# Graph network with mixtures of experts: the begins of four stages rearranged

## The chip, the cores and the metric

The kernel runs on one core of a Trainium2 chip. A core has five engines that run side by side, each taking its own instructions in order: TensorE (PE) multiplies matrices and transposes tiles, VectorE (DVE) and ScalarE (ACT) work element by element, GpSimd (POOL) issues the indirect DMAs (gathers) here, and SyncE (SP) issues most of the other DMAs; ACT and POOL have DMA queues too. PE writes to PSUM; DVE and ACT bring results from there to SBUF. The metric is the device time of one execution in microseconds (us), lower is better.

## What is computed

The input is x, 3125 nodes by 256 channels, with 50,000 edges (source, destination, one of eight types, a weight). Eight blocks follow each other, each with a residual connection and a layer norm ahead of it:

```python
x = x + L0_gnn(norm(x))      # attention over edges
x = x + L0_ffn(norm(x))      # slices and attention over them
x = x + L1_gnn(norm(x))      # four graph convolutions, 256-128-64-128-256
x = x + L1_ffn(norm(x))      # two of 16 experts per node, then a norm
x = x + L2_gnn(norm(x))      # two blocks norm-convolution-relu, then x @ Wp.T + bp
x = x + L2_ffn(norm(x))      # a shared MLP and two of 4 experts
x = x + L3_gnn(norm(x))      # relational convolution, eight edge types
x = x + L3_ffn(norm(x))      # one of 8 experts, with a capacity
```

The four convolutions of L1 gnn each form `segment_sum(h[src] * dinv[src] * dinv[dst], dst) + b`. L1 ffn, where the change has its largest part:

```python
gate_logits = x @ gate_w + gate_b
topk_vals, topk_idx = jax.lax.top_k(gate_logits, K)          # K = 2
topk_w = jax.nn.softmax(topk_vals, axis=-1)
h = jax.nn.relu(jnp.einsum('bsh,ehf->bsef', x, w1) + b1)     # 16 experts, 256 -> 512
expert_out = jnp.einsum('bsef,efh->bseh', h, w2) + b2        # 512 -> 256
sel = jnp.take_along_axis(expert_out, topk_idx[:, :, :, None], axis=2)
y = x + jnp.sum(topk_w[..., None] * sel, axis=2)
return (y - mu) / jnp.sqrt(var + EPS) * gamma + beta
```

L3 gnn forms `h_all = einsum('ni,roi->rno', node, weight)` and sums `h_all[type, src]` by destination.

## The kernel before

Nodes lie in 25 tiles (NT) of 128 (P); x stays in SBUF as 128x25x256 floats, D = 256 channels, KC = 2 chunks of 128. Many loops run over groups of five tiles (SG). A framework's scheduler sets the order of instructions on each engine and the waits between engines; the program text does not fix it, but work that depends on nothing late can be drawn forward. Stages follow each other in time: L0 up to about 400 us, the building of an edge-count table (cells) up to 720, L1 gnn 724 to 1114, L1 ffn 1114 to 1502, L2 gnn 1504 to 2250, L2 ffn to 2420, L3 gnn to 3057, L3 ffn to the end. Pools of SBUF tiles are opened and closed by stage, and a new pool's tile can only be written once its addresses' old users are done. `evict` (L103 to L105) copies PSUM to SBUF and takes ACT and DVE in turn, call by call.

L1 gnn (`l1_gnn`, L1066 to L1131). The biases b1 to b4 are loaded through SP's queue, and right after them five DVE additions add b4 to all of x (L1074). Then four calls of `aggregate` follow. In each, a tile takes 25 PE matmuls with the edge counts (L1081, PSUM tile `agg`), a DVE reduction over the three bf16 parts (L1084, `s`), and then the stage's `finish`: after1 scales and adds b1, transposes (L1090, `tr`), applies relu on ACT (L1092), multiplies by w2 and splits into three bf16 parts; after4 scales (L1123), transposes, multiplies by w4 (L1125) and adds the product to x (L1126). While a tile's finish runs, PE goes on with the next tile's matmuls.

L1 ffn (`l1_ffn`, L1154 to L1317). The expert weights w1 and w2 (16.8 MB) are loaded through SP (L1179, L1182). Then the front, by groups of five tiles (from L1186): layer norm, a store of the normed rows to the DRAM table `tab_x1` through POOL's queue (L1190), transposes (L1195), `by_node` matmuls with the gate's weights (L563), and an addition of the gate's bias into `lg` (L1199). Then routing on DVE: `top_two` (L591 to L615), counting, and the owners of the slots. Between, beta is added to x (L1247). Then the work on experts: a gather of 128 rows per slot from `tab_x1` (L681, `xg`), transposes (L1262), two layers of matmuls (L1268, L1281) and a store to `yb`.

L2 gnn (`l2_gnn`, L1325 to L1424). The weights W6, W7 and Wp are loaded into two buffers `w_o`, transposed (L1335) and copied by `evict`. Then, for each group of five tiles, `input_group` (the function `combined` of L1 ffn) loads y from `tab_x1` through SP (L1295), gathers two expert rows per tile from `yb` through POOL (`yg`, three buffers each), folds them into y (L1303), norms, and adds to x (L1311, L1313); after it `first_input` norms, transposes and multiplies by W6. The adjacency tables `adj` (1.6 MB each, L517) are loaded through SP.

L3 gnn (`l3_gnn`, L1645 to L1719). For each block of 128 edges: a gather of source rows (L681, `g`), a DVE comparison that makes a 0/1 matrix (`hot`, L1703), and PE matmuls that sum the rows by destination and type (L1708, `sum`). DVE adds each sum into a ring of destinations in SBUF (`acc`, 128x8576 floats, L1714). When a tile of destinations is complete, ACT copies it out and clears its place by a copy from `zero` (L1664, L1665), and PE multiplies it by the weights (L1685); then the front of L3 ffn follows for that tile (`l3_ffn_front`: layer norm, `f_tr`, `f_xT`, `f_mm`). At the stage's begin DVE clears `zero` (L1654) and the whole ring (L1657).

## Time and profile before

| what | us |
|---|---|
| runs before, median of 3 (lowest, highest) | 3270.08 (3268.21, 3270.93) |
| the profiled execution | 3264.51 |
| its span on the core | 3262.6 |

| engine | busy us | share of the span |
|---|---|---|
| PE (matmul) | 2693.3 | 83% |
| DVE | 1408.6 | 43% |
| ACT | 871.3 | 27% |
| POOL | 632.8 | 19% |

The busy shares are averages over stages with different limits, so the stage's own rows decide. In a timeline row the bracket at the end gives how long the engine had been idle before the row and what released it. The granted PE clock (mean 0.905 over the span) is the share of full speed that the throttle let through.

### The profile page before, as it was taken

The page shows a single profiled execution, that of the slowest core. Times are in us where ns is not written, and L with a number is a line of the kernel's source. Part 1 is how long each engine was busy: PE and PEld are TensorE (multiplying, and loading weights), DVE is VectorE, ACT ScalarE, POOL GpSimd, SP SyncE. Part 2 cuts the span into 40 slices and gives each one's busy share as a digit, 9 for nine tenths or more (in the row PEclk, how much of TensorE's full clock was granted, in tenths as well). Part 3 has the DMA queues.
Part 4 walks back from the last instruction along what each step waited for, and adds up shares of the span by engine and source line. Part 5 has one row for each costly group of instructions (what it writes and reads, how often), then busy time and mean ns, then how long its engine had stood idle before and what let it go on. Part 6 is the DMA issues. An engine that isn't in the chain of part 4 may idle for free. (4 is left out here: it accounts for less than half of the span.)

```text
span 3262.6 us, 41054 instructions
## 1 busy us (share of the span) xinstructions
PE 2693.3 (83%) x14727; PEld 2034.3 (62%) x14727; DVE 1408.6 (43%) x3870; ACT 871.3 (27%) x2259; POOL 632.8 (19%) x660
## 2 busy tenths in 40 slices
PE   4488877778999869994799999998965878878688
PEld 3255766654775556553588888885433666666555
DVE  5764888863452362223812111114342333343422
ACT  1373488871220012332200000002320121121223
POOL 2600000000000001113200000000026666665132
PEclk9797999999999859997899999998986888888799
DMA  4200232230000343335243333321014555555542
GB/s 128 53 8 1 65 137 123 122 136 4 1 1 1 129 133 86 82 83 166 73 152 142 134 141 141 133 97 47 30 54 139 145 147 152 147 148 142 208 116 51
DMA packets 160019, 326.08 MB, mean 100 GB/s; under 512 B 44757, under 2 KB 116997, under 8 KB 150186
## 3 DMA queue, kind: packets, MB, share of 16 engines
q1 hardware_dynamic: 118005, 211.51, 19.3%
q0 software_dynamic: 37472, 108.23, 11.8%
q10 hardware_dynamic: 4308, 3.40, 0.4%
q8 instruction: 126, 2.06, 0.3%
q14 instruction: 108, 0.88, 0.1%
HBM read 244.26 MB, written 79.46 MB: 99 GB/s over the span
## 5 line engine op out<-in xcount | busy, mean ns | idle before, releaser
L1420 PE MATMUL agg<-h,adj 128*128 128x256 f32 x2500 | 545.7, 379 | 0.5 <-DVE h L1378 0.4
L1420 PEld LDWEIGHTS agg<-h,adj 128*128 128x128 f32 x2500 | 473.9, 190 | 65.3 <-DVE h L1378 1.5
L681 POOL DMA_INDIRECT g<-tab,grp_src x391 | 379.6, 971 | 228.4 <-issue 90.8
L1081 PE MATMUL agg<-hs,cnt 128*128 128x384 bf16 (+1 forms) x2500 | 335.4, 288 | 16.1 <-DVE s L1084 10.7
L1708 PE MATMUL sum<-hot,g 128*128 128x192 bf16 x2346 | 273.9, 268 | 83.1 <-issue 46.6
L1708 PEld LDWEIGHTS <-g 128*128 128x128 bf16 x2346 | 225.4, 108 | 135.5 <-issue 83.3
L1685 PE MATMUL po<-wT,done 128*128 128x256 f32 x800 | 249.8, 435 | 48.0 <-ACT done L1664 25.5
L1081 PEld LDWEIGHTS <-cnt 128*128 128x128 fp8e4 x2500 | 229.8, 100 | 94.9 <-issue 20.5
L324 PE MATMUL cell_w<-rows,wgt 128*128 128x125 f32 x1280 | 208.1, 301 | 78.0 <-ACT wgt L318 78.0
L324 PEld LDWEIGHTS cell_w<-rows,wgt 128*128 128x128 f32 x1280 | 168.6, 191 | 113.1 <-ACT wgt L318 88.7
L1714 DVE TENSOR_TENSOR acc<-acc,sum 128x384 f32 x196 | 108.1, 552 | 289.1 <-remote 120.7
L1422 DVE SCALAR_TENSOR_TENSOR o<-agg,dinv,b 128x256 f32<-128x256 f32 x50 | 24.2, 484 | 437.6 <-PE agg L1420 437.6
L318 ACT ACTIVATE wgt<-one,win_w 128x128 f32<-128x128 bf16 x480 | 208.0, 520 | 4.3 <-DVE one L312 3.4
L1685 PEld LDWEIGHTS po<-wT,done 128*128 128x128 f32 x800 | 154.7, 217 | 69.4 <-ACT done L1664 29.0
L1664 ACT COPY done<-acc 128x2048 f32<-128x2048 f32 x25 | 47.5, 1899 | 416.0 <-issue 370.8
L1651 POOL IOTA iota_w<- 128x192 f32 x1 | 0.3, 302 | 805.3 <-PE mm L1485 805.3
L1268 PE MATMUL mm<-w,xgT 128*128 x240 | 122.5, 616 | 10.5 <-ACT xgT L1264 10.5
L681 POOL DMA_INDIRECT xg<-tab_x,owner_l x76 | 71.9, 947 | 299.3 <-PE tr L1262 210.1
L1281 PE MATMUL po<-w,hT 128*128 x480 | 118.4, 389 | 11.3 <-ACT hT L1277 11.2
L309 DVE TENSOR_TENSOR rows<-iota_f,win_m 128x1000 f32<-128x1000 f32 x80 | 96.0, 1200 | 52.1 <-PE cell_w L324 50.8
L1703 DVE TENSOR_SCALAR hot<-iota_n,grp_loc 128x192 bf16<-128x192 bf16 x391 | 89.1, 286 | 64.0 <-issue 27.0
L1281 PEld LDWEIGHTS po<-w,hT 128*128 128x128 f32 x480 | 86.7, 189 | 46.0 <-ACT hT L1277 35.9
(544 smaller groups left out, 3866.7 us busy)
## 6 DMA issues: line engine op xcount, KB each, us to landing
adj<-adjw SPq DMA_DIRECT2D x50, 1600.0 KB
adjw<-cells_w SPq DMA_DIRECT2D x25, 1600.0 KB
w<-in_L_ffn_w_dram SPq DMA_DIRECT2D x16, 1024.0 KB
b<-in_L_ffn_b_dram SPq DMA_DIRECT2D x76, 128.0 KB
yb<-yo SPq DMA_DIRECT2D x76, 128.0 KB
w<-in_L_ffn_w_dram SPq DMA_DIRECT2D x16, 512.0 KB
w<-in_L_ffn_w_dram SPq DMA_DIRECT2D x32, 256.0 KB
g<-tab,grp_src POOLq DMA_INDIRECT x391
```

Of the source, the lines that this page charges most:

```text
L309: nc.vector.tensor_tensor(rows, iota_f[:, None, : GN * NT].to_broadcast([P, WB, GN * NT]), win_m[:, q, None].to_broadcast([P, WB, GN * NT] ...
L318: nc.scalar.mul(wgt[:, i, :], one[:, :, i], win_w[:, g + i : g + i + 1])
L324: nc.tensor.matmul(pw[:, i // HB, c], wgt[:, i, :], rows[:, i, :], start=True, stop=True)
L681: nc.gpsimd.indirect_dma_start(out=dst, out_offset=None, in_=table, in_offset=bass.IndirectOffsetOnAxis(ap=idx, axis=0))
L1081: nc.tensor.matmul(ps[:, : 3 * m], cnt[:, k, t * P : (t + 1) * P], hs[:, k, : 3 * m], start=(k == 0), stop=(k == NT - 1))
L1268: nc.tensor.matmul(ph, xgT[:, k, :], w1[:, bass.ds(e, 1), k, :].rearrange("p e f -> p (e f)"), start=(k == 0), stop=(k == KC - 1))
L1281: nc.tensor.matmul(po, hT[:, f, :], w2[:, bass.ds(e, 1), f, :].rearrange("p e d -> p (e d)"), start=(f == 0), stop=(f == FC - 1))
L1420: nc.tensor.matmul(acc, ch[:, k, :], h[i][:, k, :], start=(k == 0), stop=(k == NT - 1))
L1685: nc.tensor.matmul(po, done[:, k, r, :], wT[:, k, r, :], start=(r == 0 and k == 0), stop=(r == NR - 1 and k == KC - 1))
L1703: nc.vector.tensor_scalar(hot[:, j, :], iota_n, grp_loc[:, s * PT + j, g : g + 1], None, op0=ALU.is_equal)
L1708: nc.tensor.matmul(ps[:, k, :], e[:, j, i * D + k * P : i * D + (k + 1) * P], hot[:, j, :], start=(j == 0 and i == 0), stop=(j == nt - 1 a ...
L1714: added.append(nc.vector.tensor_add(to, to, ps.rearrange("p k (r n) -> p k r n", r=NR)))
```

## The change

Four stages' begins are altered.

- L1 gnn: the loads of b1 to b4 go through POOL's queue. The five additions of b4 to all of x become 25 additions, one at the end of each tile's after1.
- L1 ffn: the front is a new function `l1_ffn_front` for one tile. The tile t-1's front is called at the end of tile t's after4, in the fourth aggregate, and the last tile's after it. Its copy from PSUM is always ACT's, its store to `tab_x1` goes through SP, and the addition of beta is in it. Its gate weights, bias, beta and logits lie in a pool that lives for the whole kernel. (`l1_gnn_of_any`, the branch for other graphs, which these inputs do not take, calls the front in a loop of its own.)
- L2 gnn: the three loads of weights have three buffers and are issued at once; group 0's `input_group` is called ahead of the transposes of the weights, whose copies are all ACT's; b6, b7 and bp are loaded through ACT's queue.
- L3 gnn: the ring is cleared by five copies on ACT from a zero tile that is set in the stage before.

One further line lets a small tile of L0 ffn share another's buffer ("osT" takes the name "v").

```diff
--- before.py
+++ after.py
@@ -163,6 +163,13 @@
     grp_wide = const.tile([P, 1], I32, name="grp_wide")
     dinv = const.tile([P, 2, NT], F32, name="dinv")
     slow_path = const.tile([P, 1], I32, name="slow_path")
+
+    NE1 = 16
+    tab_x1 = dram.tile([NP, D], F32, name="tab_x1")
+    lg_1 = const.tile([P, NT, NE1], F32, name="lg_1")
+    gw_1 = w_load(const, "gw_1", a["L1_ffn_gate_w"], KC, NE1)
+    gb_1 = bcast_load(const, "gb_1", a["L1_ffn_gate_b"], NE1)
+    beta_1 = bcast_load(const, "beta_1", a["L1_ffn_beta"], D)
 
     mid_stack = ExitStack()
     mid = mid_stack.enter_context(tc.tile_pool(reuse_waits="tile", name="mid", bufs=1))
@@ -887,7 +894,7 @@
         for h in range(H):
             nc.tensor.transpose(ps[:, h, :], at[:, h, :], ident[:G, :G])
         evict(atT, ps)
-        osT = mp.tile([C, H, G], F32, name="osT")
+        osT = mp.tile([C, H, G], F32, name="v")
         ps = pp.tile([C, H, G], F32, name="mm")
         for h in range(H):
             nc.tensor.matmul(ps[:, h, :], v[:, h, :], atT[:, h, :], start=True, stop=True)
@@ -1001,6 +1008,21 @@
         build_cells(cnt, sp, bp, pp)
 
 
+    def l1_ffn_front(wp, pp, t):
+        n = wp.tile([P, 1, D], F32, name="f_x")
+        layer_norm(n, x[:, t : t + 1, :], 0, 1)
+        nc.sync.dma_start(tab_x1[t * P : (t + 1) * P, :], n[:, 0, :])
+        pt = pp.tile([P, KC, P], F32, name="f_tr", bufs=1)
+        for k in range(KC):
+            nc.tensor.transpose(pt[:, k, :], n[:, 0, k * P : (k + 1) * P], ident)
+        xT = wp.tile([P, KC, P], F32, name="f_xT")
+        nc.scalar.copy(xT, pt)
+        ps = pp.tile([P, NE1], F32, name="f_mm", bufs=1)
+        by_node(ps, xT, 0, gw_1)
+        nc.vector.tensor_add(lg_1[:, t, :], ps, gb_1)
+
+        nc.vector.tensor_add(x[:, t, :], x[:, t, :], beta_1)
+
     def l1_gnn_of_any(lp, wp, ap, pp, adj1):
         w2 = lp.tile([128, 64], F32, name="w2")
         w3 = lp.tile([64, 128], F32, name="w3")
@@ -1068,10 +1090,9 @@
         w4 = lp.tile([128, D], F32, name="w4")
         for t, i in ((w2, 2), (w3, 3), (w4, 4)):
             nc.scalar.dma_start(t, a[f"L1_gnn_W{i}"])
-        b1, b2, b3, b4 = (bcast_load(lp, f"b{i}", a[f"L1_gnn_b{i}"], n) for i, n in ((1, 128), (2, 64), (3, 128), (4, D)))
+        b1, b2, b3, b4 = (bcast_load(lp, f"b{i}", a[f"L1_gnn_b{i}"], n, nc.gpsimd)
+                          for i, n in ((1, 128), (2, 64), (3, 128), (4, D)))
         hs_2 = lp.tile([P, NT, 3 * P], BF16, name="hs_2")
-        for g in range(0, NT, SG):
-            nc.vector.tensor_add(x[:, g : g + SG, :], x[:, g : g + SG, :], b4[:, None, :].to_broadcast([P, SG, D]))
 
         def aggregate(hs, m, finish):
 
@@ -1105,6 +1126,7 @@
             z = wp.tile([P, P], F32, name="z")
             nc.vector.tensor_scalar(z[:, :64], po, scale, None, op0=ALU.mult)
             in_three(hs_2, t, 64, z[:, :64], wp)
+            nc.vector.tensor_add(x[:, t, :], x[:, t, :], b4)
 
         def after2(s, t, scale):
             nc.vector.scalar_tensor_tensor(s, s, scale, b2, op0=ALU.mult, op1=ALU.add)
@@ -1125,10 +1147,14 @@
             nc.tensor.matmul(po, turned(s, 128, AF.Copy), w4, start=True, stop=True)
             nc.vector.tensor_add(x[:, t, :], po, x[:, t, :])
 
+            if t:
+                l1_ffn_front(wp, pp, t - 1)
+
         aggregate(hs_1, 128, after1)
         aggregate(hs_2, 64, after2)
         aggregate(hs_1, 64, after3)
         aggregate(hs_2, 128, after4)
+        l1_ffn_front(wp, pp, NT - 1)
 
     with tc.If(nc.values_load(slow_path[0:1, 0:1], min_val=0, max_val=1) > 0) as any_order:
         with ExitStack() as s:
@@ -1142,6 +1168,11 @@
             ap = s.enter_context(tc.tile_pool(reuse_waits="tile", name="l1a_adj", bufs=1))
             pp = s.enter_context(tc.tile_pool(reuse_waits="tile", name="l1a_ps", bufs=1, space=PSUM))
             l1_gnn_of_any(lp, wp, ap, pp, adj1)
+        with ExitStack() as s:
+            wp = s.enter_context(tc.tile_pool(reuse_waits="tile", name="l1b_w", bufs=2))
+            pp = s.enter_context(tc.tile_pool(reuse_waits="tile", name="l1b_ps", bufs=1, space=PSUM))
+            for t in range(NT):
+                l1_ffn_front(wp, pp, t)
     with any_order.Else():
         with ExitStack() as s:
             lp = s.enter_context(tc.tile_pool(reuse_waits="tile", name="l1g", bufs=1))
@@ -1158,16 +1189,13 @@
         NS = 2 * N // P + NE
         FEW = NS - 4
         more = lp.tile([P, 1], I32, name="more")
-        tab = dram.tile([NP, D], F32, name="tab_x1")
+        tab = tab_x1
         yb = dram.tile([NS * P, D], F32, name="yb1")
         zero = lp.tile([P, D], F32, name="zero")
         nc.vector.memset(zero, 0.0)
         nc.gpsimd.dma_start(yb[FEW * P :, :].rearrange("(t p) d -> p t d", p=P),
                             zero[:, None, :].to_broadcast([P, NS - FEW, D]))
-        gw = w_load(lp, "gw", a["L1_ffn_gate_w"], KC, NE)
-        gb = bcast_load(lp, "gb", a["L1_ffn_gate_b"], NE)
         gamma = bcast_load(lp, "gamma", a["L1_ffn_gamma"], D)
-        beta = bcast_load(lp, "beta", a["L1_ffn_beta"], D)
 
         with tc.tile_pool(reuse_waits="tile", name="l1f_e", bufs=1) as ep:
 
@@ -1183,21 +1211,7 @@
                                         a["L1_ffn_w2"][e : e + 2, c * P : (c + 1) * P, :].rearrange("e p d -> p e d"))
             nc.sync.dma_start(b1, a["L1_ffn_b1"].rearrange("e (c p) -> p e c", p=P))
             with tc.tile_pool(reuse_waits="tile", name="l1f_r", bufs=1) as rp, tc.tile_pool(reuse_waits="tile", name="l1f_w", bufs=2) as wp:
-                lg = rp.tile([P, NT, NE], F32, name="lg")
-                for t in range(0, NT, SG):
-                    n = wp.tile([P, SG, D], F32, name="ln_x")
-                    layer_norm(n, x[:, t : t + SG, :], 0, SG)
-                    nc.gpsimd.dma_start(tab[t * P : (t + SG) * P, :].rearrange("(t p) d -> p t d", p=P), n)
-                    ps = pp.tile([P, SG, NE], F32, name="mm")
-                    for j in range(SG):
-                        pt = pp.tile([P, KC, P], F32, name="tr")
-                        for k in range(KC):
-                            nc.tensor.transpose(pt[:, k, :], n[:, j, k * P : (k + 1) * P], ident)
-                        xT = wp.tile([P, KC, P], F32, name="xT_t", bufs=3)
-                        evict(xT, pt)
-                        by_node(ps[:, j, :], xT, 0, gw)
-                    nc.vector.tensor_add(lg[:, t : t + SG, :], ps, gb[:, None, :].to_broadcast([P, SG, NE]))
-                picks = top_two(rp, lg, NE)
+                picks = top_two(rp, lg_1, NE)
                 wts = []
                 for j, (oh, w) in enumerate(picks):
                     nc.vector.tensor_scalar(oh[:, NT - 1, :], oh[:, NT - 1, :], tail_mask, None, op0=ALU.mult)
@@ -1242,10 +1256,6 @@
                 own_r = slot_owners(rp, wp, pp, slots, NS)
                 owner = lp.tile([P, NS], I32, name="owner_l")
                 nc.vector.tensor_copy(owner, own_r)
-
-            for g in range(0, NT, SG):
-                nc.vector.tensor_add(x[:, g : g + SG, :], x[:, g : g + SG, :], beta[:, None, :].to_broadcast([P, SG, D]))
-
             def work(xp, s0, s1):
                 for s in range(s0, s1):
                     if s % NL == 0 or s == s0:
@@ -1324,18 +1334,20 @@
 
     def l2_gnn(lp, wp, ap, pp, input_group):
 
-        wts = {}
+        raw, wts = {}, {}
         for name in ("W6", "W7", "Wp"):
-            wt = wp.tile([P, KC, D], F32, name="w_o")
-            nc.scalar.dma_start(wt, a[f"L2_gnn_{name}"].rearrange("(o p) i -> p o i", p=P))
+            raw[name] = wp.tile([P, KC, D], F32, name="w_o", bufs=3)
+            nc.scalar.dma_start(raw[name], a[f"L2_gnn_{name}"].rearrange("(o p) i -> p o i", p=P))
+        input_group(0)
+        for name, wt in raw.items():
             wT = lp.tile([P, KC, D], F32, name=f"{name}T")
             for k in range(KC):
                 ps = pp.tile([P, D], F32, name="mm")
                 for o in range(KC):
                     nc.tensor.transpose(ps[:, o * P : (o + 1) * P], wt[:, o, k * P : (k + 1) * P], ident)
-                evict(wT[:, k, :], ps)
+                nc.scalar.copy(wT[:, k, :], ps)
             wts[name] = wT
-        vec = {n: bcast_load(lp, n, a[f"L2_gnn_{n}"], D) for n in ("b6", "b7", "bp")}
+        vec = {n: bcast_load(lp, n, a[f"L2_gnn_{n}"], D, nc.scalar) for n in ("b6", "b7", "bp")}
 
         col = {n: col_load(lp, n, a[f"L2_gnn_{n}"], P, KC) for n in ("ln6_g", "ln6_b", "ln7_g", "ln7_b")}
         x1 = lp.tile([P, NT, D], F32, name="x1")
@@ -1410,7 +1422,8 @@
                 nc.vector.tensor_add(x[:, g + j, :], ps, x[:, g + j, :])
 
         for g in range(0, NT, SG):
-            input_group(g)
+            if g:
+                input_group(g)
             first_input(g)
         for i, then in (("6", second_input), ("7", output)):
             for t in range(NT):
@@ -1642,7 +1655,7 @@
             for t in range(g, g + SG):
                 then(wp, pp, t)
 
-    def l3_gnn(lp, wp, xp, pp, wT, then):
+    def l3_gnn(lp, wp, xp, pp, wT, zero, then):
 
 
         NC = NR * DW
@@ -1650,11 +1663,12 @@
         wide = lp.tile([P, NC], F32, name="iota_w")
         nc.gpsimd.iota(wide, pattern=[[1, NC]], base=0, channel_multiplier=0, allow_small_or_imprecise_dtypes=True)
         nc.vector.tensor_copy(iota_n, wide)
-        zero = lp.tile([P, P], F32, name="zero")
-        nc.vector.memset(zero, 0.0)
 
         acc = lp.tile([P, KC, NR, RING + DW], F32, name="acc")
-        nc.vector.memset(acc, 0.0)
+        for c0 in range(0, RING + DW, P):
+            c1 = min(c0 + P, RING + DW)
+            nc.scalar.copy(acc[:, :, :, c0:c1].rearrange("p k r n -> p (k r) n"),
+                           zero[:, None, : c1 - c0].to_broadcast([P, KC * NR, c1 - c0]))
 
         def finished(t):
 
@@ -1753,6 +1767,8 @@
         pp = s.enter_context(tc.tile_pool(reuse_waits="tile", name="l2f_ps", bufs=2, space=PSUM))
         l3_wT = l3_weights(l3_p, wp, pp)
         l3_bias = bcast_load(l3_p, "bias", a["L3_gnn_bias"], D)
+        l3_zero = l3_p.tile([P, P], F32, name="l3_zero")
+        nc.vector.memset(l3_zero, 0.0)
         l2_ffn(lp, wp, pp, lambda t, n: l3_input(wp, l3_bias, t, n))
     with tc.If(nc.values_load(grp_wide[0:1, 0:1], min_val=0, max_val=1) > 0) as any_place:
         with ExitStack() as s:
@@ -1766,7 +1782,7 @@
             wp = s.enter_context(tc.tile_pool(reuse_waits="tile", name="l3g_w", bufs=2))
             xp = s.enter_context(tc.tile_pool(reuse_waits="tile", name="l3g_x", bufs=6))
             pp = s.enter_context(tc.tile_pool(reuse_waits="tile", name="l3g_ps", bufs=2, space=PSUM))
-            l3_gnn(lp, wp, xp, pp, l3_wT, l3_ffn_front)
+            l3_gnn(lp, wp, xp, pp, l3_wT, l3_zero, l3_ffn_front)
     l3_stack.close()
```

## The prediction

> **What bounds the kernel now.** The program occupies one core for 3262.6 us; with 1.9 us around it, the profiled execution is 3264.5 us, 5.6 us under the median of the runs shown (3270.1). TensorE (PE) is busy 83% of the span, so I looked first, in the table of 100-us windows, for stretches where it is not, and then read the timeline there. The columns of the windows: length; busy time (instructions) of PE, PE weight load, DVE, ACT, POOL; granted PE clock; DMA share; GB/s.
>
> ```profile
> 1000.00:1100.00 100.00, 99.78 (x556) 55.52 (x555) 25.37 (x60) 5.54 (x20) 0.00 (x0) 1.00 0.00 1
> 1100.00:1200.00 100.00, 67.34 (x305) 55.31 (x302) 72.37 (x258) 9.94 (x28) 4.35 (x5) 0.58 0.64 202
> 1500.00:1600.00 100.00, 48.85 (x174) 34.83 (x173) 67.99 (x230) 21.74 (x50) 49.64 (x50) 0.68 0.50 160
> 2400.00:2500.00 100.00, 43.08 (x243) 30.40 (x242) 34.64 (x82) 10.30 (x18) 55.63 (x51) 0.61 0.37 106
> ```
>
> The first window lies in the fourth aggregate: PE full, DVE three quarters free. The other three are the begins of stages, where PE is half idle and its clock low. The timeline says for what (start, duration, engine, line, operation, output<-inputs, count, idle time before and who ended it):
>
> ```profile
> 738.52 7.10 DVE L1074 TENSOR_TENSOR x<-x,b 128x1280 f32<-128x1280 f32 x5 [18.35 <-DMA b<-in_L_gnn_b_dram]
> 746.14 1.76 PE L1081 MATMUL agg<-hs,cnt 128*128 128x384 bf16 x5 [10.72 <-DVE s L1084]
> ...
> 1113.83 0.42 DVE L1126 TENSOR_TENSOR x<-mm,x 128x256 f32<-128x256 f32 x1 [1.55 <-PE mm L1125]
> ...
> 1161.14 0.57 DVE L591 TENSOR_REDUCE top<-lg 128x25 f32<-128x400 f32 x1
> ...
> 1206.03 1.01 POOL L681 DMA_INDIRECT xg<-tab_x,owner_l  x1 [50.39 <-DVE el L1254]
> ...
> 1518.32 0.42 DVE L105 COPY WpT<-mm 128x256 f32<-128x256 f32 x1 [5.08 <-PE mm L1335]
> 1519.40 0.95 POOL L681 DMA_INDIRECT yg<-yb,slot  x1 [7.05 <-DVE y L1303]
> ...
> 2421.29 9.42 POOL L681 DMA_INDIRECT g<-tab,grp_src  x1 [15.73 <-DVE zero L1654]
> 2422.55 7.21 DVE L1657 MEMSET acc<- 128x8576 f32 x1 [1.73 <-issue]
> 2431.01 0.94 POOL L681 DMA_INDIRECT g<-tab,grp_src  x1 [0.30 <-DVE hot L1703]
> 2432.77 0.66 PE L1708 MATMUL sum<-hot,g 128*128 128x192 bf16 x3 [20.48 <-DMA g<-tab,grp_src]
> ```
>
> To be seen: PE idles 10.72 us while DVE adds b4 to x ahead of the first reduction; from the last x add of L1 gnn to the first gather of its ffn are 92 us, 47 of them the front (norm, gate) and 45 routing; the fold of y waits behind the copy of Wp, and POOL 7.05 us behind the fold; the first gather of L3 takes 9.42 us, other gathers 0.95, while DVE clears the ring.
>
> **The change, part by part.**
>
> *L1 gnn, biases.* Removed before the first reduction: the five adds, 7.10 us. The changed program's order has on DVE seven of the 25 small adds ahead of the first reduction and the other 18 among tiles 0 to 2. A 128x256 add takes 0.42 us (L1126, above), so 7 x 0.42 = 2.9. All wait for b4, which now goes fourth through POOL's queue, behind the same store of the cell table; POOL's issues follow each other at 1.25 us (gathers of 2431 to 2440), against four in 2.20 us on SP, and b4 landed at 738.5 before; bounds 736 to 741, I keep 738.5. The first reduction starts at 741.4 instead of 745.5: -4.1. But PE now does 33 aggregate matmuls before its first transpose, not 55: 22 x 0.17 (3.74 us for 22, at 1098.54) = +3.7 put off. The 18 adds, 7.6 us, meet tiles 0 to 2, 14 us in which DVE, 35% busy between 750 and 800, has 9 free. But PE has only five aggregate matmuls (0.85 us) between the last of a tile and its transpose, which just cover the tile's reduction and scaling (0.56 and 0.35); an add under way when a reduction falls due holds PE up, 0.42 in each of three tiles, +1.3. Sum +0.9, taken +1; with b4's bounds and, at worst, half of the 18 adds without cover, -4 to +6.
>
> *L1 ffn, front by tile.* Removed: 46.9 us (1114.25 to 1161.14). Added in aggregate 4, whose PE is full, so each PE cycle counts: two transposes and four small matmuls per tile. The same helper shape stands in L3's stage at 3026.25 (f_tr pair 0.38) and 3027.10 (f_mm, four, next instruction 0.47 later, 0.61 if taken whole): 0.85 to 1.0, plus two changes of operand at about 0.1: 1.1 us. By 24 tiles +26; at 0.9 it is 22, and at 1.5 (f_mm waiting 0.4 for ACT's 0.37-us copy of f_xT, which three aggregate matmuls, 0.5 us, are to cover) 36. The DVE part per tile (statistics 0.43 and 0.18, reciprocal 0.15, norm 0.41, logit add 0.17, beta add 0.42) is 1.8 us, within a period of 5.03 us that holds 1.3 of DVE work; ACT adds 0.66 and is idle. Tail: the last tile's front remains after the last x add: norm chain 1.65 (the same five steps at 2413.80 to 2415.44), then from norm to logits 2.05 (3025.87 to 3027.92), +0.3: +4.0. Stores: 25 of 128 KB on SP instead of 5 of 640 KB on POOL; SP is idle then, and in order the expert weights' loads come behind the last store. They ran 1111.4 to 1167 at a DMA share of 1.06 with the stores among them; alone 16.8 MB at 380 GB/s are 44.7 us, begun some 5 us after the last x add, done 50 to 56 after it. Gathers now begin at 4.0 + 44.9 = 49 after it: just at their end, and the first experts' weights come first, so hidden; uncovered it costs 0 to 6. The beta adds, 5 x 1.48, lay in the front and are in the tiles now. Sum: -46.9 + 4.0 + 26 = -17, bounds -21 to -7.
>
> *L2 gnn, begin.* The turning (12 transposes, 3.3 us of PE; copies now all on ACT, 6 x 0.37) moves behind group 0's fold. SP issues y of group 0 first, ahead of four column loads, so y lands near 1507 and the fold follows the gathers (six at 1505.2 to 1511.4). POOL's 7.05-us stop goes; group 0, ready at 1537.3, comes up to that much sooner. What is late next: the three 1.6-MB adjacency loads are issued about 5 us sooner too, and slow the landing of the last gathers as they did (DMA saturated 1510 to 1532). Between 0 (all paced by bytes) and -10 (7.05 plus the three column loads past which y moves), nearest to the measured stop: -7. W's turned copies are wanted only by group 0's transposes, 20 us later. The three bias loads on ACT's queue issue in 0.4 each and hold up no copy that is waited for.
>
> *L3 gnn, ring.* Removed: 7.21 us of DVE. ACT does it instead: four copies of 128x2048 at 1.90 (its row of 3022.86) and one of 128x384, about 0.5: 8.1 us from about 2420.5 on, ACT being otherwise idle. The first addition into the ring can come at 2428.6, against 2436.0. Gathers at 2421.3 and then every 1.25 us let the first sum start near 2424.5 instead of 2432.8: -8.3 if the memset held the gather, 0 if the gather was slow by itself, nothing is lost as DVE's hots run meanwhile. The first gathers of other stages (1505.16: 0.94, 1206.03: 1.01) were not slow: -8.
>
> [...]
>
> Other effects: fewer helper copies turn ACT/DVE parity downstream (one piece more or less of 0.42 against 0.37 here and there): 0, bounds 1 either way. Sum: +1 - 17 - 7 - 8 = -31: 3264.5 - 31 = 3233.5, and on the runs' scale 3239.
>
> **Rivals.**
> - *The front paces aggregate 4 (slower).* DVE works in order: if each tile's chain runs end to end (old chain 2.85 from reduction to x add, norm 1.65, logits 2.05, beta 0.42 and 0.4 of hops), the period is 7.4, not 6.1. PE is then 82% busy, and a line through the windows above (67% at 0.58, 99.8% at 1.00) gives a clock of 0.77: 6.1/0.77 = 7.9 us, +2.9 x 24 = +70. Part two becomes +27, the whole +13: 3283. It decides from 2.4 us per tile. Against it: the front in a tile's step is the tile's before, whose x add is a period old, and 16 to 17 aggregate matmuls (2.8 us) stand ahead of f_tr, longer than the norm chain. [...]
> - *The same, half as bad*: 1.8 to 2.4 per tile, the whole near 0: 3268.
> - *The ring's clearing did not hold the gather*, or L3, which later waits for gathers with all 12 buffers full, does not carry the 8 us on: -23, 3247.
> - *Weights or gathers late in L1 ffn*, as the gathers of 1519 were beside bulk loads: +6, 3245.
>
> **How the numbers follow.** Chances: forecast 0.60, ring 0.15, weights 0.08, no net gain 0.06, slower 0.11. 0.2% (6.5 us) is what runs can tell from no change. Faster: 0.60 + 0.15 + 0.08 = 0.83; same 0.06; slower 0.11. The forecast's own bounds, not all at one end, are 3223 to 3258; the range reaches to the first two rivals, 3222 to 3268.
>
> **What would show it.** In the changed profile: first reduction of L1 gnn at about 741; aggregate-4 period 6.1 us at clock 1.0 (7.4 or more: the slower rival); last x add to first xg gather 49 us; POOL's stop at the begin of L2 gnn gone, and first transposes 7 us sooner after the stage's begin; first L3 gather 0.95 and first sum 4 us after the stage's begin, the lead still there at its last tile. A period above 7 us, or a first L3 gather still near 9, would make it wrong.

## The result, and the profile after

The changed kernel takes 3240.52 us (median of 4 runs, 3232.93 to 3243.10), the kernel before, beside it, 3270.51 us (median of 4): ratio 0.9909 with a 95% interval of 0.9891 to 0.9927. Forecast were 3239 us and a range of 3222 to 3268. The profiled execution took 3241.98 us, span 3240.3: 22.4 us less span than before (3262.6). The two medians differ by 30.0: the profiled execution of before lies 6.0 us under the median beside it, that of the changed kernel 1.5 over its own. So the spread between executions, several us on either side, is part of everything below. One single execution of e5 below took 8179.75 us; why is not known, and its ratio is formed without it.

The rows of the changed kernel that answer to those shown of before (timeline; start, duration, engine, line, operation, count, and in brackets the idle time before and what ended it):

```profile
742.61 2.44 DVE L1129 TENSOR_TENSOR x<-x,b 128x256 f32<-128x256 f32 x7 [17.35 <-DMA b<-in_L_gnn_b_dram]
746.16 0.47 PE L1111 MATMUL tr<-ident,s 128*128 128x128 f32 x1 [8.07 <-DVE s L1123]
...
1132.93 0.42 DVE L1148 TENSOR_TENSOR x<-mm,x 128x256 f32<-128x256 f32 x1 [1.11 <-PE mm L1147]
1137.62 0.57 DVE L598 TENSOR_REDUCE top<-lg 128x25 f32<-128x400 f32 x1
1182.47 1.00 POOL L688 DMA_INDIRECT xg<-tab_x,owner_l  x1 [442.61 <-DMA w<-in_L_ffn_w_dram]
...
1494.81 0.48 DVE L1313 SCALAR_TENSOR_TENSOR y<-yg,wt,y 128x256 f32<-128x256 f32 x1 [11.76 <-DMA y<-tab_x]
1495.56 0.95 POOL L688 DMA_INDIRECT yg<-yb,slot  x1 [2.55 <-DMA yg<-yb,slot]
...
2405.93 0.96 POOL L688 DMA_INDIRECT g<-tab,grp_src  x1 [15.76 <-DVE iota_n L1665]
2407.54 0.95 POOL L688 DMA_INDIRECT g<-tab,grp_src  x1 [0.65 <-issue]
2409.09 0.66 PE L1722 MATMUL sum<-hot,g 128*128 128x192 bf16 x3 [12.19 <-DMA g<-tab,grp_src]
```

From the last x addition to the routing's first reduction are now 4.7 us instead of 47.3 (start to start). Routing itself, to the first gather, takes 44.9 us as before. POOL's stop at the begin of L2 gnn is 2.55 us instead of 7.05. The first gather of L3 takes 0.96 us instead of 9.42, and the first sum follows 3.2 us after its start instead of 11.5.

One period of aggregate 4, from x addition to x addition, first before and then changed:

```profile
1053.49 0.42 DVE L1126 TENSOR_TENSOR x<-mm,x 128x256 f32<-128x256 f32 x1 [1.55 <-PE mm L1125]
...
1058.52 0.42 DVE L1126 TENSOR_TENSOR x<-mm,x 128x256 f32<-128x256 f32 x1 [1.55 <-PE mm L1125]
```

```profile
1053.34 0.42 DVE L1148 TENSOR_TENSOR x<-mm,x 128x256 f32<-128x256 f32 x1 [1.39 <-PE mm L1147]
...
1055.90 0.38 PE L1017 MATMUL f_tr<-ident,f_x 128*128 128x128 f32 x2
1056.12 0.65 PE L1102 MATMUL agg<-hs,cnt 128*128 128x384 bf16 x3
1056.80 0.62 PE L570 MATMUL f_mm<-gw,f_xT 128*128 128x16 f32 x4
1057.27 0.48 PE L1102 MATMUL agg<-hs,cnt 128*128 128x384 bf16 x2
...
1059.03 0.42 DVE L1148 TENSOR_TENSOR x<-mm,x 128x256 f32<-128x256 f32 x1 [1.40 <-PE mm L1147]
```

The period is 5.69 us, 0.66 more than the 5.03 of before. No PE row in it has an idle time in its bracket, and the granted clock is 1.00: the front is paid nearly in PE time alone, 0.69 us from start to start (0.22 for the two `f_tr`, 0.47 for the four `f_mm`). Small holes remain on both sides and nearly cancel: the three aggregate matmuls ahead of `f_mm` take 0.68 us instead of 0.49, because `f_mm` waits for ACT's `f_xT` (its weight load stands idle for 0.42 us until then); before, `tr` waited 0.16 us for `s`, which the front's matmuls now cover. Forecast was a period of 6.1 us.

The whole span as a ledger, from the starts of the same instructions in both profiles (us; "forecast" is the term of the sum; each number is rounded by itself):

| stretch | before | changed | difference | forecast |
|---|---|---|---|---|
| begin to first aggregate matmul | 724.6 | 730.2 | +5.6 | 0 |
| first aggregate matmul to first x addition of aggregate 4 | 268.3 | 266.6 | -1.7 | +1 |
| first to last x addition of aggregate 4 | 121.0 | 136.1 | +15.2 | +26 |
| last x addition to routing | 47.3 | 4.7 | -42.6 | -42.9 |
| routing, to first gather | 44.9 | 44.9 | 0 | 0 |
| first gather to last expert matmul | 295.1 | 299.7 | +4.6 | 0 |
| last expert matmul to first L2 result on DVE | 125.6 | 122.7 | -2.9 | -7 |
| L2 gnn's aggregates | 571.0 | 571.2 | +0.2 | 0 |
| last aggregate to L2 ffn's choice | 51.2 | 57.4 | +6.2 | 0 |
| to L3's first gather | 172.4 | 172.4 | 0 | 0 |
| L3: first gather to first sum | 11.5 | 3.2 | -8.3 | -8 |
| L3: first sum to last sum | 602.6 | 606.8 | +4.2 | 0 |
| last sum to the end | 227.2 | 224.4 | -2.8 | 0 |
| span | 3262.6 | 3240.3 | -22.4 | -31 |

So the front brings the gain, as forecast. In these two profiles the sum missed by nearly 9 us; that 3239 met the median of 3240.5 so closely is luck, in the two executions and in terms that were wrong in both directions. The experiments ask which of these rows belong to the change and which to one execution.

### The profile page after: what moved, and what is told of

The parts are those of the page before. It is cut to its first block, busy times and chain, and to the rows that moved or that the text cites. A ratio compares the mean times of both kernels' runs of the same rounds, so it can differ in the third digit from the quotient of the medians.

```text
span 3240.3 us, 41232 instructions
## 1 busy us (share of the span) xinstructions
PE 2675.4 (83%) x14727; PEld 2025.4 (63%) x14727; DVE 1414.3 (44%) x3934; ACT 895.9 (28%) x2299; POOL 624.1 (19%) x659
## 5 line engine op out<-in xcount | busy, mean ns | idle before, releaser
L688 POOL DMA_INDIRECT g<-tab,grp_src x391 | 371.1, 949 | 233.7 <-issue 91.6
L1102 PE MATMUL agg<-hs,cnt 128*128 128x384 bf16 (+1 forms) x2500 | 342.3, 289 | 5.9 <-issue 5.6
L1699 PE MATMUL po<-wT,done 128*128 128x256 f32 x800 | 239.5, 424 | 34.1 <-issue 16.0
```

The lines of the kernel that those rows point to most:

```text
L688: nc.gpsimd.indirect_dma_start(out=dst, out_offset=None, in_=table, in_offset=bass.IndirectOffsetOnAxis(ap=idx, axis=0))
L1102: nc.tensor.matmul(ps[:, : 3 * m], cnt[:, k, t * P : (t + 1) * P], hs[:, k, : 3 * m], start=(k == 0), stop=(k == NT - 1))
L1699: nc.tensor.matmul(po, done[:, k, r, :], wT[:, k, r, :], start=(r == 0 and k == 0), stop=(r == NR - 1 and k == KC - 1))
```

## The experiments

They ran in three groups of four, each on one chip with the kernel before beside it; the first group on the second chip, the next on a third, the last on a fourth. On the third chip every kernel is 4% faster (the kernel before 3130 us instead of 3259 to 3271), so times are compared through the ratio to the kernel before of the same group, and stretches of the profiles mostly within a group. Of each edit only the lines that matter are shown; notes behind # in them are added, and ... stands for lines left out. The "first cell row" is the first DVE instruction that builds the cells (`rows`). The changed kernel's own two ratios are 0.9909 (0.9891 to 0.9927) and, in the second group, 0.9898 (0.9880 to 0.9916).

**e1_late_loads.** The three loads for the front, which the changed kernel issues at its begin ahead of L0's weights, stand on SP behind them.

```diff
-    gw_1 = w_load(const, "gw_1", a["L1_ffn_gate_w"], KC, NE1)      # and gb_1, beta_1
+    gw_1 = const.tile([P, KC, NE1], F32, name="gw_1")
...
+    nc.sync.dma_start(gw_1, a["L1_ffn_gate_w"].rearrange("(k p) n -> p k n", p=P))
     with tc.If(nc.values_load(slow_path[0:1, 0:1], min_val=0, max_val=1) > 0) as any_order:
```

> The changed kernel, with the loads of the gate's weights, its bias and beta issued behind L0's weight loads on SP instead of ahead of them. Theory: these three loads push L0's weights and what hangs on them back; the first cell row (DVE) comes at 293 us as before the change instead of 299, the first aggregate matmul at 725 instead of 730, the time falls by 5 to 6 us. Rival (L0 is later for another cause, code layout or the shared buffer of osT): the first cell row stays at 299 and the time within 2 us.

Measured: ratio 0.9892 (0.9873 to 0.9910). The first cell row comes at 288.7 us, the first aggregate matmul at 721.0. But three kernels of the same group that keep the early loads have their first cell row at 296.6, 294.3 and 289.8: executions of the same begin differ by 7 us. The place nearest to the loads is steadier: the last store of an attention row is issued at 81.6 and 78.3 us in two profiles of the kernel before, at 85.2, 83.6, 82.6, 80.3, 85.0 and 82.5 us (mean 83.2) with the early loads, and at 80.2 and 82.2 with the late ones. (Third-chip profiles left out.) The first such store shows it without overlap: at 42.6 to 46.3 us in these six profiles, at 41.5 and 42.2 with the late loads, at 41.6 and 40.0 before. On SP the weights `W` of L0 gnn are issued at 31.6 us in the changed kernel, at 28.7 in e1 and at 29.2 before. So the early loads cost 2 to 3 us there; the rest of the 5.6 us differs from execution to execution. Half of the theory, then.

**e2_biases_undone.** L1 gnn's biases as before.

```diff
-        b1, b2, b3, b4 = (bcast_load(lp, f"b{i}", a[f"L1_gnn_b{i}"], n, nc.gpsimd)
+        b1, b2, b3, b4 = (bcast_load(lp, f"b{i}", a[f"L1_gnn_b{i}"], n)
...
+        for g in range(0, NT, SG):
+            nc.vector.tensor_add(x[:, g : g + SG, :], x[:, g : g + SG, :], b4[:, None, :].to_broadcast([P, SG, D]))
...
-            nc.vector.tensor_add(x[:, t, :], x[:, t, :], b4)
```

> The changed kernel with L1 gnn's biases as before: loads on SP, five additions ahead of the first reduction. Theory: the part is worth nearly nothing, because the earlier first reduction is paid back in matmuls not done ahead and in additions among the first tiles; from first aggregate matmul to the first x addition of aggregate 4 before 268.3 us, changed 266.6; undone 267 to 269, the time within 3 us of the changed kernel. Rival (the part is a loss by the late b4): 3 to 6 us faster. Rival (a gain of 5): 5 us slower.

Measured: ratio 0.9886 (0.9869 to 0.9902); the stretch from the first aggregate matmul to the first x addition of aggregate 4 takes 264.7 us, and 264.6 in e7 (below), which has the biases as before too. That is less than expected and no more than with the change (264.6 to 266.6 in ten profiles), so the small additions are worth nothing. What made the stretch shorter than the 268.3 of before is another part: with gate bias and beta loaded elsewhere, the biases no longer stand behind them on SP: they are issued 3.6 us after the first aggregate matmul, 7.3 before. The first reduction comes 16.8 us after the first aggregate matmul here, 20.9 before, with the same five additions ahead of it.

**e3_ring_memset** and **e4_ring_pieces.** The ring cleared on DVE again, whole and in 16 pieces.

```diff
-        for c0 in range(0, RING + DW, P):          # five copies on ACT
+        nc.vector.memset(acc, 0.0)                 # e3
...
+        for k in range(KC):                        # e4
+            for r in range(NR):
+                nc.vector.memset(acc[:, k, r, :], 0.0)
```

> The changed kernel with the ring cleared by one DVE memset as before. Lock theory (the memset holds the gather up): the first gather takes 9 us again, the first sum comes 8 us later after the stage's begin, the time grows by 4 to 8 us. Rival (the gather is slow by itself at the begin of a new program part): it would be slow with ACT's clearing too, which the changed profile already shows not to be so; then this kernel is no slower.

> The same with the memset cut into 16 of 128x536. [...] Time between the changed kernel and e3.

Timeline of e3, begin of L3 gnn:

```profile
2397.98 9.31 POOL L688 DMA_INDIRECT g<-tab,grp_src  x1 [15.83 <-DMA tab<-l_parts]
2399.15 7.21 DVE L1668 MEMSET acc<- 128x8576 f32 x1 [5.35 <-issue]
2407.60 0.95 POOL L688 DMA_INDIRECT g<-tab,grp_src  x1 [0.30 <-DVE hot L1714]
2409.34 0.66 PE L1719 MATMUL sum<-hot,g 128*128 128x192 bf16 x3 [20.45 <-DMA g<-tab,grp_src]
```

And of e4:

```profile
2394.14 0.96 POOL L688 DMA_INDIRECT g<-tab,grp_src  x1 [15.85 <-DVE acc L1670]
2394.32 8.42 DVE L1670 MEMSET acc<- 128x536 f32 x15
2395.76 0.94 POOL L688 DMA_INDIRECT g<-tab,grp_src  x1 [0.65 <-issue]
2397.61 0.94 POOL L688 DMA_INDIRECT g<-tab,grp_src  x1 [0.91 <-issue]
2402.86 0.48 PE L1721 MATMUL sum<-hot,g 128*128 128x192 bf16 x2 [17.82 <-DVE hot L1716]
```

With one memset the gather takes 9.31 us and ends 0.93 us after it; the four profiles with such a memset (before, e3, and e7 and e12 below) agree, 9.31 to 9.42 and 0.93 to 0.95. With the same bytes in pieces DVE clears no shorter, and gathers of 0.94 to 0.96 us go out while it does, each beside two or three pieces, 1.6 to 1.9 us from start to start instead of 1.25. So it is the single long instruction that holds the gather, not the clearing as such. At what point of its work the gather stands is not shown: its row begins 1.2 to 1.3 us ahead of the memset, longer than a gather takes alone. In e4 the first sum is nevertheless late, 8.7 us after the first gather instead of 3.1 (e1 and e2): it now waits for DVE's `hot`, which stands behind the pieces. At the stage's end the picture is nearly even: from first gather to last sum e3 takes 613.4 us, e4 603.6, and the two kernels of the group with ACT's clearing 603.8 and 601.6. Ratios 0.9921 (0.9908 to 0.9935) and 0.9908 (0.9891 to 0.9925). Either way of not stopping the gathers serves, and here it was worth 10 us. Elsewhere less was left of the 8 us at the stage's end: on the fourth chip 610.1 to 611.9 in three kernels against 612.0 of the kernel before, on the third 496.4, 496.7 and 501.8 against 501.9 with a memset (e7).

**e5_stores_by_pool.**

```diff
-        nc.sync.dma_start(tab_x1[t * P : (t + 1) * P, :], n[:, 0, :])
+        nc.gpsimd.dma_start(tab_x1[t * P : (t + 1) * P, :], n[:, 0, :])
```

> The changed kernel with the 25 stores to tab_x1 through POOL's queue, so that the expert weights' loads on SP do not stand behind the last store. Theory (the 7 us lost between the first gather and the first expert matmul come from the weights' bulk loads, begun 5 us late and still filling the DMA engines): the loads begin at the end of the last aggregate matmuls, 4 to 5 us sooner against the last x addition (2.5 us after it now, 1 to 3 before it here), the first expert matmul comes 7 to 10 us after the first gather instead of 13.4, time 3 to 5 us less. Rival (the wait is the gathers' own, or the weights wait for addresses that come free later): loads begin no sooner or the 13.4 us stay.

It looked for the 7 us between the 13.5 us from first gather to first expert matmul in the changed kernel and the 6.1 before. A miss. The first two weight loads are issued 4.7 us sooner, but the next group only at 1115.44, where the changed kernel on this chip (e8) has it at 1114.81; first gather to first expert matmul stays 12.9 us (13.1 there), ratio 0.9910 (0.9891 to 0.9930). The stores ahead of them are not what the loads wait for.

**e9_pe_order** looked for the same 7 us on another engine. In the changed kernel's PE rows (timeline):

```profile
1188.38 0.69 PE L1272 MATMUL tr<-ident,xg 128*128 128x128 f32 x2 [7.29 <-DMA xg<-tab_x,owner_l]
1189.62 0.69 PE L1272 MATMUL tr<-ident,xg 128*128 128x128 f32 x2 [0.55 <-DMA xg<-tab_x,owner_l]
1190.51 0.66 PE L1272 MATMUL tr<-ident,xg 128*128 128x128 f32 x2 [0.20 <-DMA xg<-tab_x,owner_l]
1193.95 0.66 PE L1272 MATMUL tr<-ident,xg 128*128 128x128 f32 x2 [2.79 <-DMA xg<-tab_x,owner_l]
1194.95 0.66 PE L1272 MATMUL tr<-ident,xg 128*128 128x128 f32 x2 [0.34 <-DMA xg<-tab_x,owner_l]
1195.94 2.05 PE L1278 MATMUL mm<-w,xgT 128*128 x2 [0.32 <-issue]
```

Five pairs of transposes, each behind its gather, stand ahead of the first expert matmul; before there were two. The scheduler chose this order for the changed program.

```diff
+                    with tc.issue_after(first[s - s0 - 2].ins) if s0 + 2 <= s < s0 + 8 else nullcontext():
                         for k in range(KC):
                             nc.tensor.transpose(ps[:, k, :], xg[:, k * P : (k + 1) * P], ident)
```

> The changed kernel, with PE held to the order of the kernel before at the begin of the expert work: the transposes of slot s (2 to 7) stand behind the first matmuls of slot s-2. In the changed kernel five pairs of transposes stand ahead of the first expert matmul, so it waits for five gathers. Theory (the order costs what the late gathers do not): first expert matmul 8 to 9 us after the first gather, not 13.1; last expert matmul 2 to 5 us sooner after it. Rival (the weights' loads are what ends last): the first expert matmul stays near 13 us after the first gather.

```profile
1183.61 1.00 POOL L688 DMA_INDIRECT xg<-tab_x,owner_l  x1 [441.04 <-DMA w<-in_L_ffn_w_dram]
1189.40 0.69 PE L1274 MATMUL tr<-ident,xg 128*128 128x128 f32 x2 [7.17 <-DMA xg<-tab_x,owner_l]
1190.67 0.69 PE L1274 MATMUL tr<-ident,xg 128*128 128x128 f32 x2 [0.58 <-DMA xg<-tab_x,owner_l]
1191.62 3.75 PE L1280 MATMUL mm<-w,xgT 128*128 x4 [0.27 <-DMA b<-in_L_ffn_b_dram]
```

The first expert matmul comes 8.0 us after the first gather, and the last 295.3 us after it (298.8 to 301.0 in the ten profiles with the order of the changed kernel, 295.1 and 293.9 before). The order cost 4 of the 4.6 us. What is left in the 8.0 against the 6.1 of before is the first gather's landing, 5.8 us to the first transpose instead of 4.0, beside the last weights: in the changed kernel, where the landing takes 5.9, the DMA share is 1.31 and 1.26 in the two 4 us of 1181 to 1189, and 0.10 in the 4 us from 1204 on in which the first gathers of before begin. Ratio 0.9890 (0.9870 to 0.9910): 4 us is less than the times resolve.

**e6_l2_begin_undone.** L2 gnn's begin as before: two buffers, biases on SP, `evict`, group 0 after the turning.

```diff
-        input_group(0)
-        for name, wt in raw.items():
+        for name in ("W6", "W7", "Wp"):
+            wt = wp.tile([P, KC, D], F32, name="w_o")
```

> The changed kernel with the begin of L2 gnn as before. From the first yg gather to the first aggregate's result on DVE it took 121.6 us before and 119.1 changed. Theory (the part is worth 2 to 3 us here, less than forecast, because y's load waits behind the weights' loads and lands at +9 us): 121 to 123 us, the time 2 to 3 us above the changed kernel. Rival (worth the forecast 7 us): 126 us.

Measured: first fold 12.4 us after the first gather, where the changed kernel of the same group has 8.6; first L2 result after 118.3 us instead of 115.0; ratio 0.9915 (0.9900 to 0.9931) against 0.9898, that is 4.7 us of medians, with intervals that overlap. By these two the part is worth 3 to 5 us. The stretch itself varies nearly as much: on this chip e5, whose L2 begin is the changed kernel's, takes 112.4 us, and e7, which has it as before, 121.9.

**e10_l2_loads_early.** W6, W7, Wp, the biases and columns loaded during the expert work.

```diff
                     st = nc.sync.dma_start(yb[s * P : (s + 1) * P, :], yo)
+                    if s == 20:
+                        with tc.issue_after(st.ins):
+                            l2_loads()
```

> The changed kernel with the loads of W6, W7, Wp, the biases and the norm columns of L2 gnn issued among the expert work, behind the store of slot 20, into tiles of their own. Theory (in the changed kernel y and the first gathers share the DMA engines with these 1.2 MB, which is why the first fold comes 9 us after the first gather): first fold 4 to 6 us after the first gather, the first aggregate result of L2 gnn 3 to 5 us sooner after it (115 in the second profile), time 3 to 5 us less. Rival (paced by the gathers and the adjacency loads): no sooner.

A miss: first fold 7.5 us after the first gather, first L2 result after 119.2 us, where e9 of the same chip, without the early loads, has 7.7 and 118.3. But the edit moved more than the small loads. With these and the column loads out of the way, the three adjacency loads of 1.6 MB are issued 0.7 us after the first gather, where e9 has the first of them 8.7 us after it and the kernel before 8.2; they now take the place beside y and the gathers. So what the small loads alone cost is not shown; ratio 0.9898 (0.9879 to 0.9918).

**e7_front_alone.** The kernel before with the front by tile only (the other three parts as in its own lines; diff as shown for e2, e3 and e6).

> The kernel before with the front by tile alone; the other three parts as before. From the traces: the front removed is -42.6, aggregate 4 +15.2, late experts +4.6: -23 against the kernel before, -20 to -26 on its time less what the early loads cost (0 to 6): ratio 0.992 to 0.995. Forecast's sizing (aggregate 4 +26): -17 and less, ratio 0.995 to 0.997, with an aggregate-4 period of 6.1 us instead of 5.69.

Measured: ratio 0.9921 (0.9905 to 0.9937), 3105.39 us against 3130.25: -24.9 us, within the 20 to 26 expected from the traced terms, where the whole change has -30.8 in the same group. Aggregate 4 takes 136.1 us, period 5.69, as in every kernel with the front.

**e8_changed_again** and **e12_before_again.** The two kernels as they are, second profiles.

> The changed kernel as it is, a second profile. What differs between the two profiles is chance and belongs to no part of the change. Theory: the first cell row (299.2 then) falls within 289 to 297, as in the other kernels with the same begin, and L3's length from first gather to last sum (610) within 602 to 610; the stretch from the last aggregate of L2 gnn to L2 ffn's choice is 51 or 57 us, according to where the granted clock comes back. Rival (the late begin is the early loads' doing alone): 299 again.

> The kernel before, a second profile, to set beside those of this chip: whether the first cell row of a kernel with the early loads comes later than its own (theory: 1 to 6 us later; rival: no later), and how long L3 gnn and the stretch at L2 ffn's begin take without the change.

On the third chip e8's first cell row came at 278.3 us and L3 took 496.4 us, both outside what was expected: the chip is another. On the fourth, e12's first cell row is at 296.8, e9's and e10's with the early loads at 302.4 and 297.4, that of e11 (below), with the late loads, at 291.9: later by 5.5 and 0.6 with the early loads, within what one execution differs from another. The stretch at L2 ffn's begin is 51.2 and 53.1 us in the two profiles of before, and with the change in whole or part 51.3, 51.5, 53.9, 54.7, 54.9 and, in the other seven, 57.3 to 58.1. e2 and e1, same group, in windows of 6 us from 18 us (e2) and 24 us (e1) after their last L2 aggregate on (length; busy time and count of PE, PE weight load, DVE, ACT, POOL; granted clock; DMA share; GB/s):

```profile
2187.90:2193.90 6.00, 4.00 (x17) 2.73 (x15) 1.49 (x3) 1.01 (x3) 0.00 (x0) 0.54 0.33 90
2193.90:2199.90 6.00, 5.73 (x41) 4.68 (x41) 2.38 (x8) 1.81 (x4) 0.00 (x0) 1.00 0.00 0
```

```profile
2189.90:2195.90 6.00, 5.73 (x22) 4.11 (x20) 2.50 (x9) 1.76 (x3) 0.00 (x0) 0.50 0.00 0
2195.90:2201.90 6.00, 6.00 (x24) 4.86 (x24) 0.12 (x1) 0.78 (x2) 0.00 (x0) 0.50 0.00 0
```

At the same place, 24 us after the last aggregate, e2 has the full clock and does 41 matmuls in 6 us; e1 stays at half for two windows more and does 22 and 24, though PE is busy nearly all the time. That is the 6 us. In all fourteen profiles the length of this stretch goes with the clock. The half clock lasts a whole number of steps of 3.41 us here, 4 and 5 in the two of before (13.65 us in the first), 4 to 8 in the others (23.89 in the changed kernel's first); and the stretch takes 51.2 to 51.5 us where the full clock is back 23.5 us after the last aggregate, 53.1 and 53.9 where it is back at 27 to 28, 54.7 and 54.9 at 30, and 57.3 to 58.1 at 37. Why the clock comes back so late is open: no edit of the four parts that was tried decides it (e7, e6 and e2 contain the front; e7 and e2 are short, e6 long). Nor does it hang on which engine copies: with the front ACT makes the 128x512 copies and DVE the 128x128 copies of this stretch, at 0.59 and 0.29 us, the other way round than before (0.27 and 0.69), in the short ones as in the long.

**e11_together.** e1, e9 and e10 in one kernel.

> The changed kernel with both of these and the late loads of e1. If the three add up: 6 to 12 us faster than the changed kernel, ratio to the kernel before 0.986 to 0.988. If they hide one another or the experts' pace takes the gain back: 0.989 to 0.991.

Ratio 0.9898 (0.9878 to 0.9917): no better than the changed kernel by what the times can tell. Its profiled span, 3223.4, is shorter than e9's 3237.9 and e10's 3236.9, but 10.5 us of that lie ahead of the first cell row for e9 and 5.5 for e10. A version that clearly beats the changed kernel was not found.

## Why the prediction was right

The direction and the main cause came out, and the front carries most of the gain (e7). That the median came out to 1.5 us is luck, as said. Step by step:

- *L1 gnn, biases, +1*: right that it is worth nothing (e2): the first reduction comes 14.7 us after the first aggregate matmul instead of 20.9, more than the 4 us gained that were forecast there, and the stretch is no shorter for it. The step left out that taking two loads out of SP's queue ahead of the biases brings 3 to 4 us at the same place.
- *Front by tile, tail*: -42.9 forecast, -42.6 measured.
- *Front by tile, aggregate 4, +26*: mis-sized; +15.2, 0.63 us per tile instead of 1.1. The step took f_tr at its recorded 0.38, f_mm at its recorded 0.61 rather than at the 0.47 to the next instruction, which it had too, and added "two changes of operand at about 0.1"; in the changed kernel the next instruction starts 0.22 us after f_tr and 0.47 us after f_mm, so the two cost 0.69. No run shows a term for a change of operand, and nothing is left for it in these starts. The same 0.22 stood in the timeline that the step was read from: there the next PE row starts at 3026.47, after f_tr at 3026.25.
- *Front by tile, loads and experts, 0 (0 to 6)*: the size, +4.6, lies in the range given, but the mechanism named, weights or gathers late, holds for little of it; it was the order in which the scheduler put five transposes ahead of the first matmul (e9). It could have been read in the changed program's PE order before.
- *Loads moved to the kernel's begin*: not costed at all. They cost 2 to 3 us in L0 (e1 and the other profiles).
- *L2 gnn, -7*: right mechanism, mis-sized; 3 to 5 us by e6 and the first two profiles. The step took y to land at 1507, 3 us after its issue; in the changed profile it is 9.7 us from issue to first fold (1485.13 to 1494.81), and POOL's stop shrank to 2.55 us rather than to nothing. The adjacency loads, which the step had 5 us sooner, come later: 10.7 us after the first gather instead of 8.2. What y waits for is open; e10 took the small loads away but put the adjacency loads in their place.
- *L3, ring, -8*: the first sum came 8.3 us sooner, and e3 and e4 show the cause given, the memset: beside the whole one, of 7.21 us, the first gather takes 9.31 us, beside the pieces 0.96. How much of it reaches the stage's end differs: 10 us in the first group of experiments, 4 in the first pair of profiles, 0 to 2 on the fourth chip, 0 to 5 on the third.
- *Slower rival*: it did not occur. No PE row of aggregate 4's period has an idle time in its bracket, clock 1.00, period 5.69.
- *No term*: from the last sum of L3 to the end eleven of the twelve profiles with the front, e7 among them, take 224.1 to 224.9 us (e5 226.9), the two of before 227.2 and 227.0; the cause is open.

In the ledger aggregate 4 is 11 us cheaper than forecast, L1 gnn and the end together 5 or 6. Against that stand +5.6 at the begin, +4.6 at the experts, +6.2 at L2 ffn's clock, +4 in L3's course, and 4 less gained at L2 gnn's begin: 24 us that the sum did not have. These two profiles therefore show 22 us where 31 were forecast.

## What to carry to other kernels

Work moved under a full engine cost here nearly what the next instruction's start shows in the trace (0.69 us per tile, 0.63 in the ledger), not the recorded durations (0.38 and 0.61), and it took 42.6 us off the path for a price of 15.2. A step that only moved loads still had a price on the queue it was put ahead of (2 to 3 us in L0, e1), and the scheduler answered by another order on an engine that the edit does not touch (4 us, e9): read that order beside the diff. One long DVE instruction beside a row of gathers (here 7.21 us, the first gather 9.31) can be cut into pieces or given to ScalarE; beside either the first gather took 0.96.

## What was not expected of the hardware

The chips differ in one stage far more than elsewhere. On the third chip L3 gnn takes 496 to 502 us from first gather to last sum, on the others 602 to 614; in the changed kernel's two profiles that is 113.6 of the 140.6 us between the spans (3240.3 and 3099.7). (The first cell row comes some 20 us sooner there as well, 278.3 against 299.2.) In windows of 100 us in its middle (columns as above), first the changed kernel on the third chip, then on the first:

```profile
2600.00:2700.00 100.00, 84.54 (x670) 67.92 (x670) 47.51 (x151) 22.64 (x21) 75.63 (x81) 1.00 0.63 178
```

```profile
2700.00:2800.00 100.00, 77.19 (x548) 64.59 (x549) 37.50 (x121) 18.75 (x18) 61.89 (x66) 0.86 0.52 147
```

On the third chip POOL issues 81 gathers, one every 1.23 us, the pace of gathers that wait for nothing (1.25 in e3's rows), at a PE clock of 1.00, and PE's idle time ahead of the sums ends with a gather's landing (58.7 of 59.8 us in 2450 to 2850). On the first it issues 66, at a clock of 0.86, with PE idle where the profile shows nothing that it waits for ("issue", 46.6 us ahead of the sums in the kernel before). What withholds the instructions there was not tried. And the granted clock can stay at 0.50 for 12 us of which PE is busy 11.7 (e1 above). In the same stretch of the kernel before (2207.5 to 2221.2 us) it rose after a step of 3.41 us in which PE was busy for 2.93; in the changed kernel (2189.1 to 2213.0) it did not after one with 3.14 us of work and two that PE filled, and only the next one, filled too, ended the half clock. What it rises on is not shown.
